# A four-layer graph network on one core: feature sums, weight sums and final additions given other places, some of them fixed, in the kernel's list of work

## The chip, the cores and the metric

The kernel runs on one core of one Trainium2 chip. The metric is the device time of one execution in microseconds (us). Before the change it is 2921.49 us, the median of four executions (2918.78 to 2921.88). The engines are PE (TensorE, matrix products), DVE (VectorE), ACT (ScalarE), POOL (GpSimd) and SP (SyncE, which here only issues DMAs); each works through a queue of its own in order.

## The reference, cut to what matters

There are N = 2708 nodes with 512 features in fp32 and one dense matrix `adj` of 2708 x 2708. Every layer multiplies a matrix made from `adj` with the features, and ends in a layernorm with a residual:

```python
x = _layernorm(x + _L0_gnn_ref(x, adj))        # (adj + row-normalised mask) @ x / degree
x = _layernorm(x + _L1_gnn_ref(x, adj, adj, ...))  # attention and GCN branch, gates
x = _layernorm(x + _L2_gnn_ref(x, adj, weight))
x = _layernorm(x + _L3_gnn_ref(x, adj, deg, W, b))

def _L2_gnn_ref(x, adj_norm, weight):
    out = x @ weight[0]
    p = x
    for idx in range(1, 4):
        p = adj_norm @ p
        out = out + p @ weight[idx]
    return out

def _L3_gnn_ref(x, adjacency, node_degree, W, b):
    dinv = jax.lax.rsqrt(node_degree)
    pooled = (dinv * (adjacency + eye) * dinv) @ x + x
    return jax.nn.relu(pooled @ W + b)
```

## The kernel before

**Tiling.** Each of the large products is cut into 2 x 2 blocks (two halves of 1354 nodes, two halves of 256 features) and done with seven block products in place of eight (Strassen's method in Winograd's form). That needs sums of blocks on both sides: for the features B11, B12, B21, B22 the sums T1 = B12 - B11, T2 = B22 - T1, T3 = B22 - B12 and T4 = B21 - T2, and for the matrix tiles the sums s1 to s4. All these sums are DVE instructions; the passes of the block products are PE's. In layers 0 and 1 the sums of the features are made once, whole, by `x_sums` (L220, L221, L223) and `x_last`, while the tiles of the layer before are still being normalised. The sums of the matrix tiles are made as the tiles arrive from memory (L396 there).

**Stages.** `S[0]` to `S[6]` are the starts of seven sweeps in a common list. Sweeps 0, 1 and 2 are done by `sweep` over ranges of 384, 384, 256 and 330 columns. Sweeps 3, 4 and 5 (the three hops of layer 2) and 6 (layer 3) are done by `sweep2`: it has two halves g of 676 and 678 columns, and in each of them seven products j = 0 to 6, each of 2 units of the list. A product is seven runs of passes (L1154), each run over 6 tiles of 128 rows in sweeps 3 to 5 and over 5 in sweep 6. Its runs use b11, t3, t1, t2, t4, b22 and b21 as the stationary side. The seven runs go into four PSUM banks: `accu`, `accc`, `accd`, `acca`. DVE needs, for one product: the sums s3, s1, s2 and the last one of the streamed tiles (`comb`, L1114); the sums t3, t1, t2, t4 of the stationary side (`tsum`, L1135, two instructions each); the additions that take the banks away (`leave`, L1178, with copies by ACT, L1172); additions among the products' results (`add`, L1190).

**The rest.** 1354 rows are 10 tiles of 128 and 74 more. The 74 last rows of both halves are multiplied on their own (`rest`, L1225 and L1229): eight passes into four banks `accr`, twice in the fourth product (j = 3) and twice in the sixth (j = 5) of half 0, and likewise in half 1. `rest_add` (L1236) adds the four banks to results on DVE, and that is what makes the banks free again. There are 8 PSUM banks in all.

**Other sums.** `ext_sums` makes the sums s1 to s4 of the transposed features that hop 2 and the others append to the matrix tiles (the sixth tile of a run): four loads from X2T by SP, four DVE sums (L1080), four stores by POOL's queue. It is called eight times, four in the sweep of S[2] and four in that of S[3].

**The end.** `done6` finishes layer 3. For the end group it takes the eight quarters (s, c) of the last product's result and does three DVE instructions on each (`pre`, L1334 to L1336: add the transposed features, multiply by the row factor, add again), then 6 tiles of dense products with the output weights (`ps_d`, L599), the bias and relu (L1359, L1360), and a layernorm (L548 to L558, with the power by POOL at L553).

**What sets the order.** Every piece of work is put into the list `events` by `at(pos, fn, hold)`. The list is sorted by `pos` and run, so that it gives the program's order. A scheduler then reorders the instructions of each engine by its own estimates, within the data dependences. Two things bind it: instructions before position START = 5.0 keep their order, and those of a `fn` recorded with `hold` are tied behind the instruction that stands before them in the list on their engine. The ties make no wait on another engine by themselves; they fix who stands behind whom in an engine's queue:

```python
p = last if n < 3 * strict else done if n in held else {}
if i.engine in p:
    tc.add_manual_dep(i, p[i.engine].name, ...)   # NoSync: "order of the list"
```

`x_sums`, `x_last` and `pre` are held before the change; `comb`, `tsum`, `leave`, `add`, `rest`, `rest_add` and `ext_sums` are not.

Of the kernel before, what the change touches and what calls it, by code (L numbers as in the profile page):

```python
# [24 lines left out]
ALU = mybir.AluOpType  # L25
P = 128
# [32 lines left out]
def wt(k):  # L59
    return min(P, NH - k * P) if k < KT else P  # L60
# [8 lines left out]
def gnn_kernel(ctx: ExitStack, tc: tile.TileContext, x, adjT, w_sa, a_sa, w_gcn, b_gcn, wab, bab, w_hop, w_out,  # L69
               b_out, out):  # L70
    nc = tc.nc
# [3 lines left out]
    HD = D // 2  # L75
# [41 lines left out]
    def feature(nm):  # L117
# [11 lines left out]
    X2T = {(g, h): dram.tile([D, 2 * n], F32, name=f"X2T{g}_{h}", tag=f"X2T{g}_{h}")  # L129
           for g, (_, n) in enumerate(RANGES2) for h in range(2)}  # L130
# [4 lines left out]
    SE = {(m, g, s): dram.tile([HD, n], F32, name=f"E{m}{g}{s}", tag=f"E{m}{g}{s}")  # L135
          for m in SUMS for g, (_, n) in enumerate(RANGES2) for s in range(2)}
# [4 lines left out]
    def move(queue, dst, src):  # L141

        m = dst.shape[0]
        c = m - m % 16 if m > 16 else m
        queue.dma_start(out=dst[:c], in_=src[:c])
        if c < m:
            queue.dma_start(out=dst[c:m], in_=src[c:m])

    def ring_tile(nm):
        return pool.tile([P, 384], F32, name=nm, tag="ring", bufs=RING)  # L150
# [21 lines left out]
    def at(pos, fn, hold=False):  # L172

        def go():
            n = len(nc.cur_bb.bb.instructions)
            fn()
            held.update(range(n, len(nc.cur_bb.bb.instructions)))

        events.append((pos, len(events), go if hold else fn))


    X = {}
# [8 lines left out]
    def new_x(s, k):  # L191
        X[s, k] = place(s, *HOME[k])
        return X[s, k]

    def place(s, g, i):
        if (s, g) not in groups or i in groups[s, g][1]:
            group(s, g)
        t, used = groups[s, g]
        used.add(i)
        return t if g == "R" else t[:, i, :]  # L200
# [12 lines left out]

    b12 = {}

    def x_sums(k):
        w = wt(k)
        b = b12.pop(k)
        b11, b22 = X["B11", k], X["B22", k]
        nc.vector.tensor_tensor(new_x("T1", k)[:w], b[:w], b11[:w], ALU.subtract)  # L220
        nc.vector.tensor_tensor(new_x("T2", k)[:w], b22[:w], X["T1", k][:w], ALU.subtract)  # L221
        X["T3", k] = b
        nc.vector.tensor_tensor(b[:w], b22[:w], b[:w], ALU.subtract)  # L223
        X.pop(("B12", k), None)
# [5 lines left out]
    def b12_tile(k):  # L230

        b12[k] = place("T3", *HOME[k])
        return b12[k]

    def x_source(src, k):

        lo, hi = src[k], src[KT + k]
        return lo[:, :HD], lo[:, HD:], hi[:, :HD], hi[:, HD:]

    def x_load(src, k, s, eng):  # L240
        w = wt(k)
        q = x_source(src, k)[("B11", "B12", "B21", "B22").index(s)]
        t = b12_tile(k) if s == "B12" else new_x(s, k)
        move(eng, t[:w], q)

    def next_x(base, src, sums=0.95, halves=-0.25):


        q = nc.gpsimd
        at(base + 1.3, lambda: rest_x(src, q))  # L250
        for k in range(KW):
            f = k / KT
            if (k * P) < RANGES[-1][0]:
                at(base - 5.8 + f, lambda k=k: x_load(src, k, "B11", q))
                at(base - 1.85 + f, lambda k=k: x_load(src, k, "B22", q))
                at(base - 1.84 + f, lambda k=k: x_load(src, k, "B12", q))
                at(base - 1.15 + f, lambda k=k: x_sums(k), True)
                at(base - 0.85 + f, lambda k=k: x_load(src, k, "B21", q))
                at(base + 1.5 + f, lambda k=k: x_last(k), True)
            else:  # L260
                at(base + halves + 0.05 * (k - 8), lambda k=k: x_load(src, k, "B22", q))
                at(base + max(halves, 0.1) + 0.05 * (k - 8), lambda k=k: x_load(src, k, "B21", q))
                at(base + sums + 0.03 * (k - 8), lambda k=k: x_sums(k), True)
                at(base + 2.6 + 0.03 * (k - 8), lambda k=k: x_last(k), True)
# [345 lines left out]
    S = [28.0 * s for s in range(8)]  # L610
# [172 lines left out]
    for k in range(KW):  # L783
        f = k / KT
# [80 lines left out]
    i = 0  # L865
# [200 lines left out]
            move(nc.gpsimd, o[b : b + m, :], src[t][a : a + m, :])  # L1066
        return o

    def ext_sums(g, s, q):

        n = RANGES2[g][1]
        E = {}
        for ij in ("11", "21", "22", "12"):
            E[ij] = ring_tile("a" + ij)
            e = (int(ij[1]) - 1) * HD + q * P
            nc.sync.dma_start(out=E[ij][:, :n], in_=X2T[g, int(ij[0]) - 1][e : e + P, s * n : (s + 1) * n])
        E["s3"] = ring_tile("s3")
        for m, o, a, b, op in (("s3", "s3", "11", "21", ALU.subtract), ("s1", "21", "21", "22", ALU.add),
                               ("s2", "11", "21", "11", ALU.subtract), ("s4", "12", "12", "11", ALU.subtract)):
            nc.vector.tensor_tensor(E[o][:, :n], E[a][:, :n], E[b][:, :n], op)  # L1080
            nc.gpsimd.dma_start(out=SE[m, g, s][q * P : (q + 1) * P, :], in_=E[o][:, :n])

    def sweep2(base, ext, done, extra=None):
        nk = K2 + ext
        u = 2 / 7
        for g, (i0, n) in enumerate(RANGES2):
            Q, C = {}, {}
            for j, m in enumerate(ORDER2[g]):
                b = base + 14 * g + 2 * j
                op, st = OPS2[m]  # L1090
# [46 lines left out]
                for nm, x, y, pos in (("t3", "b22", "b12", -0.9), ("t1", "b12", "b11", 0.1), ("t2", "b22", "t1", 0.9),  # L1137
                                      ("t4", "b21", "t2", 1.9)):
                    if g == j == 0:
                        pos = max(pos, 0.4)  # L1140
                    at(b + u * pos, lambda a=(nm, x, y), f=tsum: f(*a))

                def stat(v, k, T=T, st=st):
                    i, kk = k // 3, k % 3
# [12 lines left out]
                for i, (v, z, home, start) in enumerate((  # L1157
                        ("b11", (0, 0), "u", 1), ("t3", "s3", "c", 1), ("t1", (1, 0), "d", 1), ("t2", (0, 0), "u", 0),
                        ("t4", (1, 1), "c", 0), ("b22", (0, 0), "d", 0), ("b21", (0, 1), "a", 1))):
                    for k in range(nk):  # L1160
# [3 lines left out]
                src, dst = {(0, "Q6"): ("Q1", "Q1"), (0, "Q4"): ("Q1", "Q1"), (1, "Q6"): ("Q1", "U"), (1, "Q7"): ("U", "V"),  # L1164
                            (1, "Q4"): ("V", "V"), (1, "Q3"): ("U", "U"), (1, "Q2"): ("Q1", "Q1")}.get((g, m), (None, m))
# [72 lines left out]
            for j, pos, h, e, to in REST2[g]:  # L1238
                b = base + 14 * g + 2 * j
# [13 lines left out]


    for i in range(4):
        at(S[2] + 19.5 + 1.1 * i, lambda i=i: ext_sums(0, i // 2, i % 2))
        at(S[3] + 7.0 + 1.3 * i, lambda i=i: ext_sums(1, i // 2, i % 2))

    def hop_done(dst):

# [56 lines left out]
    def done6(p0, dp, g, i0, n, h, cc, tiles):  # L1317
        def rows(s):
            row[g, h, s] = ring_tile("row")
            nc.gpsimd.dma_start(out=row[g, h, s][:, :n], in_=bcast(DROW[h][0:1, i0 + s * n : i0 + (s + 1) * n], n))  # L1320

        x3T = {}

        end = (g, h) == (1, 0)

        def load_x3T(s, c):
            t = ring_tile("x3T")
            nc.gpsimd.dma_start(out=t[:, :n], in_=X3T[g, h, s][c * P : (c + 1) * P, :])
            x3T[s, c] = t

        def pre(s, c):
            t = x3T[s, c]
            y = cc(s, c)
            nc.vector.tensor_tensor(y[:, :n], y[:, :n], t[:, :n], ALU.add)  # L1334
            nc.vector.tensor_tensor(y[:, :n], y[:, :n], row[g, h, s][:, :n], ALU.mult)
            nc.vector.tensor_tensor(y[:, :n], y[:, :n], t[:, :n], ALU.add)  # L1336

        for s in range(2):
            at(p0 - (1.9 if end else 0.6), lambda s=s: rows(s))
            for c in range(DC):  # L1340
                if end:
                    a = p0 - 1.8 + 0.05 * c
                    b = p0 - 1.5 + 0.2 * (c - 2) + 0.4 * s if c >= 2 else p0 + {
                        (1, 1): -0.9, (1, 0): -0.6, (0, 1): -0.3, (0, 0): -0.07}[s, c]
                else:
                    a, b = p0 - 0.5 + 0.4 * s + 0.05 * c, p0 + 0.4 * s + 0.05 * c
                at(a, lambda s=s, c=c: load_x3T(s, c))
                at(b, lambda s=s, c=c: pre(s, c), True)
        for i, (s, lo, w) in enumerate(tiles[3:] + tiles[:3] if end else tiles):
            got = {}  # L1350
            r0 = i0 + s * n + lo

            def a(r0=r0, w=w, got=got):
                got["x"] = fetch2(X3, h, r0, w)

            def b(s=s, lo=lo, w=w, r0=r0, got=got):
                px = dense(lambda c: cc(s, c)[:, lo : lo + w], W[6], w)
                y = got["x"]
                nc.vector.tensor_tensor(px[:w], px[:w], vec[6][:w], ALU.add)  # L1359
                nc.vector.scalar_tensor_tensor(y[:w], px[:w], 0.0, y[:w], ALU.max, ALU.add)  # L1360
                layernorm([(y, 0, D)], y, w, True)
                move(nc.sync, out[h * NH + r0 : h * NH + r0 + w, :], y[:w])

            p = p0 - 0.095 + 0.14 * i if end else p0 + 0.4 + 0.25 * i
            at(p - 0.6, a)
            at(p, b)

    sweep2(S[6], 0, done6)

    strict = 0  # L1370
# [53 lines left out]
```

## Time and profile before

| | |
|---|---|
| median of four executions | 2921.49 us |
| the profiled execution's own time | 2921.88 us |
| its span, first to last instruction | 2919.8 us |
| PE busy | 2862.9 us, 98% of the span |
| DVE busy | 2236.2 us, 77% |
| POOL busy | 660.3 us, 23% |
| ACT busy | 579.5 us, 20% |
| mean granted TensorE clock | 0.995 |

The profile gives, for one execution, the busy time of each engine, groups of instructions by source line, the waits of each engine with what ended them, and a timeline of single instructions. Times inside the execution count from its first instruction. A line such as L1154 is a line of the kernel before; names such as `z` and `t` are the program's tiles with their numbers left out. A table of windows gives the busy time of each engine in a stretch, how many instructions it holds, and PEclk, the clock that TensorE was granted there (1.00 is full speed).

### The profile page before, as it was taken

The page shows a single profiled execution, that of the slowest core. Times are in us where ns is not written, and L with a number is a line of the kernel's source. Part 1 is how long each engine was busy: PE and PEld are TensorE (multiplying, and loading weights), DVE is VectorE, ACT ScalarE, POOL GpSimd, SP SyncE. Part 2 cuts the span into 40 slices and gives each one's busy share as a digit, 9 for nine tenths or more (in the row PEclk, how much of TensorE's full clock was granted, in tenths as well). Part 3 has the DMA queues.
Part 4 walks back from the last instruction along what each step waited for, and adds up shares of the span by engine and source line. Part 5 has one row for each costly group of instructions (what it writes and reads, how often), then busy time and mean ns, then how long its engine had stood idle before and what let it go on. Part 6 is the DMA issues. An engine that isn't in the chain of part 4 may idle for free. (4 is left out here: it accounts for less than half of the span.)

```text
span 2919.8 us, 37394 instructions
## 1 busy us (share of the span) xinstructions
PE 2862.9 (98%) x10846; PEld 1844.0 (63%) x10846; DVE 2236.2 (77%) x5676; ACT 579.5 (20%) x1133; POOL 660.3 (23%) x1178
## 2 busy tenths in 40 slices
PE   7999999999999999999999999999999999999998
PEld 5655665556665656866666666666666666655664
DVE  6898788566648675875789788887888878689887
ACT  4554200101137454651100000000000200100001
POOL 0133224113310101123113033030330413512202
PEclk9999999999999999999999999999999999999999
DMA  7665466444534333565677677576775776956652
GB/s 224 187 206 183 134 212 221 133 154 157 182 117 138 117 114 100 170 194 152 204 207 224 200 208 235 153 219 193 221 221 151 223 206 182 260 163 178 182 163 90
DMA packets 376248, 523.96 MB, mean 179 GB/s; under 512 B 64454, under 2 KB 326640, under 8 KB 376044
## 3 DMA queue, kind: packets, MB, share of 16 engines
q1 hardware_dynamic: 305688, 370.70, 43.6%
q0 software_dynamic: 53376, 139.76, 14.9%
q10 hardware_dynamic: 16980, 11.13, 1.4%
q8 instruction: 86, 1.41, 0.2%
q14 instruction: 118, 0.97, 0.1%
HBM read 432.14 MB, written 89.21 MB: 179 GB/s over the span
## 5 line engine op out<-in xcount | busy, mean ns | idle before, releaser
L1114 DVE TENSOR_TENSOR z<-z 128x339 f32<-128x339 f32 (+1 forms) x966 | 457.1, 504 | 15.0 <-PE accu L1154 3.8
L1172 ACT COPY q<-accu 128x338 f32<-128x338 f32 (+1 forms) x84 | 34.5, 443 | 986.5 <-PE accu L1154 986.5
L1154 PE MATMUL accu<-z,t 128*128 128x338 f32 (+1 forms) x644 | 195.8, 450 | 6.1 <-DVE q L1178 3.1
L1154 PE MATMUL accc<-s,t 128*128 128x338 f32 (+1 forms) x644 | 198.0, 450 | 0.0
L1154 PE MATMUL accc<-z,t 128*128 128x338 f32 (+1 forms) x644 | 196.1, 451 | 0.0
L1154 PE MATMUL accd<-z,t 128*128 128x338 f32 (+1 forms) x644 | 193.8, 448 | 1.4 <-DVE z L1114 1.4
L553 POOL TENSOR_TENSOR rstd<-rstd,neg_half 128x1 f32<-128x1 f32 (+3 forms) x92 | 62.2, 676 | 580.9 <-DVE rstd L552 578.2
L1275 POOL DMA_DIRECT2D Y<-y x192 | 105.2, 554 | 367.3 <-DVE y L1270 337.9
L396 DVE TENSOR_TENSOR a<-a,a 128x384 f32<-128x384 f32 (+2 forms) x330 | 161.6, 511 | 15.0 <-PE accu L451 14.4
L1154 PEld LDWEIGHTS accu<-z,t 128*128 128x128 f32 x644 | 122.1, 191 | 68.1 <-DVE z L1114 3.9
L1154 PEld LDWEIGHTS accc<-z,t 128*128 128x128 f32 x644 | 122.7, 192 | 62.3 <-issue 4.0
L1154 PEld LDWEIGHTS accd<-z,t 128*128 128x128 f32 x644 | 122.0, 190 | 62.8 <-DVE z L1114 1.9
L1154 PEld LDWEIGHTS accc<-s,t 128*128 128x128 f32 x644 | 120.3, 190 | 64.1 <-issue 8.3
L1114 DVE TENSOR_TENSOR s<-z 128x338 f32<-128x338 f32 (+1 forms) x322 | 150.3, 504 | 12.3 <-PE accc L1154 8.4
L1178 DVE TENSOR_TENSOR q<-q,accd 128x338 f32<-128x338 f32 (+1 forms) x112 | 56.3, 503 | 128.2 <-PE accd L1154 128.2
L972 ACT ACTIVATE e<-row,neg_s 128x384 f32<-128x384 f32 (+5 forms) x176 | 100.4, 571 | 80.1 <-DVE e L974 25.4
L974 DVE TENSOR_TENSOR e<-e,f 128x384 f32<-128x384 f32 (+5 forms) x176 | 87.5, 506 | 28.5 <-ACT f L973 27.8
L973 ACT ACTIVATE f<-row,neg_s 128x384 f32<-128x384 f32 (+5 forms) x176 | 100.0, 568 | 24.4 <-PE accc L451 5.1
L599 PE MATMUL ps_d<-w,q 128*128 128x512 f32 (+2 forms) x192 | 86.2, 595 | 1.8 <-DVE ld L1360 1.3
L399 POOL DMA_DIRECT2D As<-a x120 | 64.9, 544 | 93.1 <-DVE a L396 78.1
L890 DVE SCALAR_TENSOR_TENSOR deg<-a,deg 128x384 f32<-128x384 f32 (+2 forms) x152 | 75.4, 504 | 13.3 <-DMA a<-in_adjT 12.1
L975 DVE SCALAR_TENSOR_TENSOR a<-a,e 128x384 f32<-128x384 f32 (+2 forms) x160 | 80.2, 507 | 4.1 <-DMA a<-in_adjT 1.9
(609 smaller groups left out, 5933.6 us busy)
## 6 DMA issues: line engine op xcount, KB each, us to landing
z<-As SPq DMA_DIRECT2D x320, 169.5 KB
z<-As SPq DMA_DIRECT2D x320, 169.0 KB
a<-in_adjT SPq DMA_DIRECT2D x240, 192.0 KB
z<-in_adjT SPq DMA_DIRECT2D x240, 169.5 KB
z<-in_adjT SPq DMA_DIRECT2D x240, 169.0 KB
a<-in_adjT SPq DMA_DIRECT2D x120, 165.0 KB
a<-in_adjT SPq DMA_DIRECT2D x112, 128.0 KB
As<-a POOLq DMA_DIRECT2D x60, 192.0 KB, 3.5
```

The costliest lines, as they stand in the source:

```text
L396: nc.vector.tensor_tensor(A[r, dst, k][:, :n], A[r, a, k][:, :n], A[r, b, k][:, :n], op)
L399: nc.gpsimd.dma_start(out=SD[m][k * P : (k + 1) * P, R0 : R0 + n], in_=A[r, dst, k][:, :n])
L553: nc.gpsimd.tensor_tensor(rstd[:w, 1:2], rstd[:w, 0:1], neg_half[:w], ALU.pow)
L599: nc.tensor.matmul(o, lhs(c), r, start=c == 0 and n == 0, stop=c == DC - 1, skip_group_check=True)
L890: nc.vector.scalar_tensor_tensor(d[:w, :n], a[:w, :n], 0.0, d[:w, :n], ALU.not_equal, ALU.add)
L972: nc.scalar.activation(e[:w, :n], row[R0, h][0][:w, :n], AF.Exp, bias=neg_s[:w, t : t + 1])
L973: nc.scalar.activation(f[:w, :n], row[R0, h][1][:w, :n], AF.Exp, bias=neg_s01[:w, t : t + 1])
L974: nc.vector.tensor_tensor(e[:w, :n], e[:w, :n], f[:w, :n], ALU.min)
L975: nc.vector.scalar_tensor_tensor(a[:w, :n], a[:w, :n], 0.0, e[:w, :n], ALU.not_equal, ALU.mult)
L1114: nc.vector.tensor_tensor(d[:, :n], Z[x + (k,)][:, :n], Z[y + (k,)][:, :n], op)
L1154: nc.tensor.matmul(B[home][:, :n], stat(v, k), a[:, :n], start=bool(start and k == 0), stop=k == nk - 1, skip_group_check=True)
L1275: nc.gpsimd.dma_start(out=rows[:, :, f * P : (f + 1) * P], in_=o[32 * f : 32 * (f + 1), : m * P].rearrange("p (b d) -> p b d", d=P))
```

## The change

It has four parts, and no instruction is added or removed: the number of instructions of every engine is the same.

1. **Feature sums of a layer** (`next_x`): `x_sums` is cut in two. The first of the three sums, T1 (L220), becomes `x_first` and is put, for the eight tiles of the ranges before the last, at `base - 2.3` in place of `base - 1.15`; it stays held. The loads of B12 go from `base - 1.84` to `base - 3.2`.
2. **Extension sums** (`ext_sums`): the four loads stay at their place; the four sums come 0.9 units later and are held; the four stores come 0.9 units later.
3. **Sums of the dense side** (`tsum`): held in half 0 for the products j = 0 to 3, in sweeps 3 to 6. Their positions don't change.
4. **The final additions** (`pre` of `done6`, for the end group): (0, 2), (1, 2), (0, 3), (1, 3) go from `p0 - 1.5`, `-1.1`, `-1.3`, `-0.9` to `p0 - 0.5`, `-0.7`, `-0.4`, `-0.65`, and (1, 1) from `p0 - 0.9` to `p0 - 0.75`. The three others stay.

```diff
+    def x_first(k):
+        w = wt(k)
+        nc.vector.tensor_tensor(new_x("T1", k)[:w], b12[k][:w], X["B11", k][:w], ALU.subtract)
+
+    def x_sums(k, first=True):
         w = wt(k)
+        if first:
+            x_first(k)
         b = b12.pop(k)
...
-                at(base - 1.84 + f, lambda k=k: x_load(src, k, "B12", q))
-                at(base - 1.15 + f, lambda k=k: x_sums(k), True)
+                at(base - 3.2 + f, lambda k=k: x_load(src, k, "B12", q))
+                at(base - 2.3 + f, lambda k=k: x_first(k), True)
+                at(base - 1.15 + f, lambda k=k: x_sums(k, False), True)
...
+        at(pos, loads)
+        at(pos + 0.9, sums, True)
+        at(pos + 0.9, stores)
...
-                    at(b + u * pos, lambda a=(nm, x, y), f=tsum: f(*a))
+                    at(b + u * pos, lambda a=(nm, x, y), f=tsum: f(*a), g == 0 and j < 4)
...
-        at(S[2] + 19.5 + 1.1 * i, lambda i=i: ext_sums(0, i // 2, i % 2))
-        at(S[3] + 7.0 + 1.3 * i, lambda i=i: ext_sums(1, i // 2, i % 2))
+        ext_sums(S[2] + 19.5 + 1.1 * i, 0, i // 2, i % 2)
+        ext_sums(S[3] + 7.0 + 1.3 * i, 1, i // 2, i % 2)
...
-                    b = p0 - 1.5 + 0.2 * (c - 2) + 0.4 * s if c >= 2 else p0 + {
-                        (1, 1): -0.9, (1, 0): -0.6, (0, 1): -0.3, (0, 0): -0.07}[s, c]
+                    b = p0 + {(1, 1): -0.75, (1, 2): -0.7, (1, 3): -0.65, (1, 0): -0.6, (0, 2): -0.5, (0, 3): -0.4,
+                              (0, 1): -0.3, (0, 0): -0.07}[s, c]
```

## The prediction

> **What bounds the kernel now.** I read the page's first part, then PE's waits, then the windows around each wait, and last the timeline of DVE there. PE is busy 98% of the span, so time can be won only where PE stands still or runs at half clock, and be lost wherever a sum now comes too late for it. The waits of PE (engine, line, what it waited for, us in total, times, longest):
>
> ```profile
> PE accr L1225 <- DVE q L1236: 4.7, 2, 4.4
> PE ps_n L582 <- DVE P1c L512: 3.9, 1, 3.9
> PE accu L1154 <- DVE q L1178: 3.1, 1, 3.1
> PE accd L1154 <- DVE z L1114: 3.0, 5, 1.4
> PE accu L1154 <- DVE z L1114: 3.0, 1, 3.0
> ```
>
> Each of them is a wait for DVE, which is busy 77% on the whole: DVE does the right work in the wrong order. The reader is to see single long waits, not many short ones. What a long wait costs besides is in the windows (PE's busy time, then PEclk, the granted clock):
>
> ```profile
> 439.10:442.51 3.41, 1.11 (x4) 0.36 (x2) 3.41 (x11) 0.00 (x0) 1.50 (x4) 1.00 0.98 358
> 442.51:445.92 3.41, 1.80 (x6) 1.27 (x7) 3.41 (x10) 0.00 (x0) 3.41 (x7) 0.50 0.44 126
> 445.92:449.34 3.42, 3.42 (x10) 2.10 (x9) 3.09 (x6) 0.00 (x0) 3.42 (x7) 0.50 0.79 266
> ```
>
> After a stretch of 3.41 us in which PE was busy 1.11 us, two stretches run at half clock. The same follows at 374.25 (busy 1.49), 1534.78 and 2558.78 (busy 1.50), but not at 2872.80 (busy 1.66, idle 1.75). So I price a half-clock stretch at half of what PE was busy in it, and say that it comes from about 1.9 us of idle in a stretch.
>
> The Trainium skill, "TensorE: Matmul & The Clock Gate", Part 1, says that the clock falls after at least one idle window of about 3.4 us. By that rule none of the stretches above (idle at most 3.27 us, at 1534.78) would halve the clock, my three terms for it (0.9, 1.7 and 1.7 us) would be nothing, and the sum below would be 4.3 us less. The rows speak against it, and they decide.
>
> **Part 1, feature sums, 440 us.** PE waits 3.91 us (440.21 to 444.12) for P1c (L512), which DVE reaches at 443.58. Between 428.8 and 441.7 DVE does seven of the T1 sums (L220) at a pitch of 0.335 us, 2.35 us in all. They move to 404 to 416, where DVE is busy 9.48 of 12 us and waits 2.42 us at 410.24; their inputs are there by then, because the loads' queue (POOL) keeps its order. Then P1c comes about 2.0 us sooner and the wait is 1.9 us. Loss at half clock now: (1.80 + 3.42)/2 = 2.6 us; 1.9 us of idle is on the edge, so one such stretch may stay, and I count 0.9 (bounds 0 and 2.6). Together 2.9 us.
>
> **Part 2, extension sums, 1533 us.**
>
> ```profile
> 1520.09 0.51 DVE L1178 TENSOR_TENSOR q<-q,accd 128x338 f32<-128x338 f32 x1 [1.11 <-PE accd L1154]
> 1525.91 0.51 DVE L1080 TENSOR_TENSOR s<-a,a 128x339 f32<-128x339 f32 x1 [5.31 <-DMA a<-X2T]
> ...
> 1537.49 1.75 DVE L1236 TENSOR_TENSOR q<-q,accr 128x338 f32<-128x338 f32 x4
> ```
>
> DVE stands 5.31 us behind a sum whose loads have not landed, with everything else queued behind it, and so frees the bank of the rest 4.43 us too late. With the sums 0.9 units (about 11 us) later and tied there, DVE is 3 to 5 us earlier at L1236 (1532.6 to 1534.3) and the wait goes. With it goes a half-clock stretch in which PE was busy 3.50 us: 4.43 + 1.7 = 6.1 us. The four stores also come later on POOL's queue; POOL is busy 4.18 of 4.50 us at 1533.6 and 2.42 of 3.50 after, and their reader, the next half of the hop, is far. In layer 2's last range (1280 to 1330) the same tie, and the order that the scheduler builds around it, makes DVE wait some 8 us for `accd` (L512); counting 45 sums at 0.43 us after that, the sum C21 reaches PE 0.3 us late. I count -0.3.
>
> **Part 3, stationary sums held.** This cuts both ways.
>
> Gain, sweep 6. At 2535 to 2565 DVE is late for two PE waits, 1.39 us at 2555.08 and 3.00 at 2560.28:
>
> ```profile
> 2540.45 0.43 DVE L1135 TENSOR_TENSOR t<-B11D,B11B 128x256 f32<-128x256 f32 x1 [4.90 <-DMA B11D<-X]
> ...
> 2547.47 0.51 DVE L1178 TENSOR_TENSOR q<-q,accu 128x338 f32<-128x338 f32 x1 [2.81 <-ACT q L1172]
> ```
>
> The t3 sum, unheld, stands ahead of the leaves and waits 4.90 us for its load; then ACT's copy, behind a slow store, costs 2.81. Held, t3 goes behind the leave of `accd` (PE done at 2545.3), and the layernorm chain ahead of it no longer waits for t sums. Laid end to end from 2545.3 at the pitches of the timeline (0.42 for a 338-column sum, 0.87 for 768 columns, 0.47 and 0.34 for t), the z sums are ready 0.65 us late for the first wait and, with PE taking seven passes of the next banks ahead, 0.9 us late for the second. The 0.59 us at 2504.68 goes too. Gaps: 0.6 + 0.7 + 2.1 = 3.4. Half clock now: (2.33 + 3.41)/2 = 2.9; 0.65 + 0.9 = 1.55 us of idle is below the 1.75 that kept full clock, but not by much, so I count only the longer stretch, 1.7 (bounds 0 and 2.9). Together 5.1 us. If ACT's copy stays late, the second wait stays 3.0 and 3.8 of this is gone.
>
> Loss, the start of the fourth product in sweeps 3 to 6, where the rest runs. Now, in sweep 3:
>
> ```profile
> 1467.55 0.51 DVE L1178 TENSOR_TENSOR q<-q,accd 128x338 f32<-128x338 f32 x1 [0.85 <-PE accd L1154]
> 1467.97 0.55 DVE L1135 TENSOR_TENSOR t<-T2C,T2A 128x384 f32<-128x384 f32 x1
> ...
> 1470.30 2.19 DVE L1114 TENSOR_TENSOR s<-z 128x338 f32<-128x338 f32 x5
> ...
> 1476.38 1.75 DVE L1236 TENSOR_TENSOR q<-q,accr 128x338 f32<-128x338 f32 x4
> ```
>
> In the new order the leaves and even the first L1236, which must wait for PE's eighth rest pass (1474.7), stand ahead of s3. DVE stands still for some 3 us before it. s3 comes at 1475.7, PE wants it at 1475.3: 0.5 us. Then the second L1236, which frees the bank of the last rest pass, stands behind ten s and z sums (0.42 us each) and four t sums (0.47): 14 instructions after the first, done at 1481.75, where PE arrives at 1480.35: 1.4 us. The 0.26 us wait at 1463.00 goes. Net 1.65 us, and the same rows stand in sweeps 4 and 5 (waits of 0.26 at 1830.68 and 2191.94); in sweep 6, by the same count, 1.55. Sum 6.5 us. The two idle times lie 4.8 us apart, so I expect no half clock. Bounds: 0, if PE's passes are enough ahead, and 2 x 1.7 us more per boundary if the clock falls.
>
> At the other product starts (j = 1, 2) the first s3 is ready 4.8 us before PE wants it (in sweep 4: 1787.1 against 1791.9). Held sums cost nothing there; that cover is what the second rival takes away.
>
> **Part 4, the end.** PE waits 0.84 us at 2886.00 for a z sum (L1114), and the six passes before it take 2.34 us where six later ones take 1.87, since DVE deals z sums and final additions in turn. With nine of these additions behind the z sums, PE reaches the 48 output passes (0.43 us each, 20.9 us, no waits) 0.8 + 0.6 = 1.4 us sooner, and DVE's last needed addition is done by 2890.0 instead of 2891.3. After them all is a chain, so 1.4 us is won (bounds 0 and 1.5). The 3.09 us wait at 2874.46 is behind POOL's power (L553); nothing moves there.
>
> **Sum.** 2.9 + 6.1 - 0.3 + 5.1 - 6.5 + 1.4 = 8.7 us. From the profiled execution's own 2921.88 us (span 2919.8) that gives 2913.2; its own time lies 0.4 above the median of the runs, which I leave out.
>
> **Rivals.**
> 1. **No difference that can be measured: 2918.** The clock stays low behind the shorter waits (0.9 and 1.7 us less) and in sweep 6 ACT's copy is still late (2.1 less): 8.7 - 4.7 = 4.0. For it: 1.9 us of idle stands at the edge, and POOL's stores set that copy. Against it: DVE's waits for t go in any case. Chance 0.25.
> 2. **Slower: 2930.** The held t sums make DVE wait for `accd` at each of the other held product starts as well, and s3 comes late. It decides from 4.8 us of delay; then the second stall of 1.4 us comes at some 12 more starts, 17 us: 2913.2 + 17 = 2930. For it: a tied instruction holds up all that stands behind it, as L1080 does above for 5.31 us. Against it: those starts have no rest, so no L1236 stands in the queue. Chance 0.10.
> 3. **The boundaries cost nothing: 2906.7.** DVE and PE make up the 1.65 us by waits that go elsewhere. Chance 0.15; the forecast has 0.50.
>
> **How the numbers follow.** About 0.2%, 5.8 us, is what a measurement of this kernel can tell from no change, so "faster" means below 2916.1 (from the profiled time). The forecast's own spread reaches over that bound with about 0.05 of the chance: faster 0.45 + 0.15 = 0.60, same 0.05 + 0.25 = 0.30, slower 0.10. The range, 2906 to 2920, holds the forecast and rivals 1 and 3 and leaves out the slower one.
>
> **What will show it.** Right: PE's wait for L1236 at about 1533 gone; the wait for P1c about 2 us; no half clock at 1538; first output pass 1.4 us sooner relative to the last products; new PE waits of 0.5 and 1.4 us at `accc` L1174 and `accr` L1245 (the new numbers of L1154 and L1225) once in each of sweeps 3 to 6. Wrong: new waits at j = 1 and 2, half clock in sweeps 3 to 6, or DVE waiting for DMA at the moved extension sums.

## The result, and the profile after

The changed kernel takes 2924.76 us (median of 34 executions, 2920.77 to 2929.67), the kernel before 2920.65 us (55 executions); the ratio is 1.0017, 95% interval 1.0012 to 1.0022. That is 3.5 to 6.4 us slower, where 8.7 us faster was forecast, and above the range of 2906 to 2920. It is just inside the 0.2% that I had named as what a measurement of this kernel can tell from no change. The profiled execution took 2925.11 us with a span of 2923.2.

PE's waits in the changed kernel, in the columns of the waits shown before (the page's own line of busy times first):

```profile
PE 2861.9 (98%) x10846; PEld 1841.4 (63%) x10846; DVE 2235.9 (76%) x5676; ACT 579.8 (20%) x1133; POOL 659.6 (23%) x1178
```
```profile
...
PE accu L1174 <- DVE q L1198: 3.6, 1, 3.6
PE accr L1245 <- DVE q L1256: 3.5, 4, 1.1
PE accc L1174 <- DVE s L1134: 3.0, 3, 1.0
PE rs L711 <- DVE run L698: 2.3, 1, 2.3
...
PE ps_n L588 <- DVE P1c L518: 1.5, 1, 1.5
PE accc L1174 <- ACT q L1192: 1.4, 1, 1.4
```

The waits that the change aims at are gone or short: 4.4 us for L1236 (now L1256) at 1533, 3.9 us for P1c, now 1.5. In their place stand new ones: 1.0 us for a streamed sum and 1.1 us for the bank of the rest, three times each (sweeps 3, 4 and 5), 2.3 us for the row sums of layer 2 (`rs`), 1.4 us for a copy by ACT in sweep 6. These are lines of PE in the changed kernel at 440 us, behind it, and at 1533 us (no wait):

```profile
439.32 0.73 PE L588 MATMUL ps_n<-ident,P1c 128*128 128x128 f32 x2 [1.55 <-DVE P1c L518]
...
452.61 1.56 PE L457 MATMUL accu<-a,B11D 128*128 128x384 f32 x4 [0.67 <-DVE B11D L566]
...
485.22 0.27 PE L854 MATMUL ps_r<-ident,rdeg 128*3 128x128 f32 x1 [0.72 <-DVE s L846]
...
1535.30 2.44 PE L1245 MATMUL accr<-r,B11R 116*128 116x338 f32 x8
```

To see what each place costs, I matched every PE pass of one trace with the pass of the same tiles in the other and read how far it is shifted. The shift is flat between the places that matter, so its steps are a ledger in us (minus is earlier), the forecast beside it:

| place | forecast | measured |
|---|---|---|
| up to 400 us, nothing changed there | 0 | -2.4 |
| layer 0 to 1 (440) | -2.9 | -2.9 |
| layer 2's last range (1260 to 1340) | +0.3 | +4.9 |
| fourth product of sweeps 3, 4, 5 | +1.65 each | +3.7 each |
| rest of sweep 3 (1533) | -6.1 | -6.4 |
| sweep 6 (2500 to 2610) | -5.1 + 1.55 | -2.5 |
| the end (2870 on) | -1.4 | +1.6 |
| sum | -8.7 | +3.4 |

The last pass of PE is 3.3 us later; the other -0.1 is in steps below 0.4. The difference of the spans is 3.4. The first row is how two executions differ where their work and order are the same: one and then no half-clock stretch near 100 and 378 us where the profile before has two and one.

### The profile page after: what moved, and what is told of

It is laid out like the page before. It is cut to its first block, busy times and chain, and to the rows that moved or that the text cites. A ratio compares the mean times of both kernels' runs of the same rounds, so it can differ in the third digit from the quotient of the medians.

```text
span 2923.2 us, 37397 instructions
## 1 busy us (share of the span) xinstructions
PE 2861.9 (98%) x10846; PEld 1841.4 (63%) x10846; DVE 2235.9 (76%) x5676; ACT 579.8 (20%) x1133; POOL 659.6 (23%) x1178
## 4 chain that ended last, share of the span: by engine, by line
PE 84%; DVE 6%; issue 4%; DMA 3%; POOL 1%; ACT 1%; SPq 0%; POOLq 0%; DVEq 0%; ACTq 0%
PE accu L1174 11%; PE accd L1174 11%; PE accc L1174 11%; PE ps_d L605 9%; PE accc L457 8%; PE accd L457 8%; PE accu L457 7%; PE acca L1174 5%; PE acca L457 4%; PE accr L1245 2%; DVE z L1134 1%; PE accr L1249 1%; PE acca L466 1%; PE accd L466 1%; PE ps_t L594 1%
## 5 line engine op out<-in xcount | busy, mean ns | idle before, releaser
L1192 ACT COPY q<-accu 128x338 f32<-128x338 f32 (+1 forms) x84 | 34.5, 443 | 994.7 <-PE accu L1174 897.0
```

## The experiments

In these kernels one part is undone or done alone. Where a time is given as a ratio, it is to the kernel before, run on the same chip in the same session, with its 95% interval. The changed kernel (1.0017, 1.0012 to 1.0022) did not run again beside them, so it is compared by way of these ratios; and the traces are of several chips, on which the kernel before took 2920.65 to 2924.89 us.

**Each part undone.** Four kernels, the changed one with one part put back: `x_sums` whole at `base - 1.15` and the B12 loads at -1.84; `ext_sums` in one piece at `pos`; `tsum` without hold (its edit is shown); `pre` at the old positions.

```diff
-                    at(b + u * pos, lambda a=(nm, x, y), f=tsum: f(*a), g == 0 and j < 4)
+                    at(b + u * pos, lambda a=(nm, x, y), f=tsum: f(*a))
```

> The changed kernel with part 1 undone (the T1 sums of the features back at their old place). Theory A (every part has its own place, and what the two traces show there adds up): the wait for P1c at 440 us is back at about 3.9 us with its half-clock stretches, and the time is 2.9 us above that of the changed kernel. Theory B (what follows in a sweep moves with the feature sums, so that the gain is given back later): within 1 us of the changed kernel.

Measured: 1.0030 (1.0018 to 1.0041), 0.13% (3.8 us) above the changed kernel, the intervals overlapping. The wait for P1c is back at 4.2 us. The shift against the changed kernel's trace is +4.3 us at that place, of which 1.8 go again by 490, where two waits of 0.7 us that part 1 had brought (lines at 452 and 485 above) are absent. That leaves +2.5. Theory A.

> The changed kernel with part 2 undone (extension loads, sums and stores together again, not held). Theory A: the 4.9 us lost between 1260 and 1340 go (DVE no longer waits 7.7 us for ACT there, and the 2.3 us wait of PE for the row sums is gone), and the 6.4 us won at 1533 go as well, so the time is about 1.5 us above the changed kernel. Theory B (the loss at 1260 to 1340 comes of part 1, whose order puts PE 5 us ahead of DVE): the loss stays, and the time is 6 us above the changed kernel.

Measured: 1.0033 (1.0020 to 1.0045). The row sums' wait falls from 2.3 to 0.4 us and the wait for L1256 at 1535 is 3.2 us again, with half clock behind it: the shift goes by -4.2 us at 1250 to 1330 and by +6.4 from 1330 to 1545. So both the loss in layer 2 and the gain at 1533 are part 2's, as theory A says. The time alone doesn't decide: it is 0.16% or 4.7 us above the changed kernel, A said 1.5 and B 6, and the intervals overlap. In the trace 1.7 us more come in sweep 4 and 3.5 in sweep 6, where part 2 moves nothing.

> The changed kernel with part 3 undone (the t sums free for the scheduler in all sweeps). Theory A (the tie is the cause of the new waits at the fourth product): the new waits of 0.6, 1.0 and 1.1 us in sweeps 3, 4 and 5 go, 3 times 3.7 us; the gain of sweep 6 (2.5 us) goes too: 8 to 9 us below the changed kernel. Theory B (those waits come of DVE being late from part 2's tie, not from part 3): they stay in sweep 3 and the time is 2 us or less below the changed kernel.

Measured: 0.9975 (0.9965 to 0.9986), 0.42% or about 12 us below the changed kernel. The new waits in sweeps 3 to 5 are gone, and the shift falls by 3.6 us at each. Theory A, but it is more than A's 8 to 9 us, and the trace doesn't show where the rest is: three times 3.6 us are 10.8, and sweep 6 gives back 2.5 of them, as A said.

> The changed kernel with part 4 undone (the final additions at their old places). Theory A (part 4 wins 1.4 us at the end, and the loss there in the profiled execution, 1.4 us of half clock after a wait of 3.6 us, belongs to POOL's order and to where the clock's stretches fall): the time is 1 to 1.5 us above the changed kernel, and PE waits 0.8 us for a z sum near the end again. Theory B (part 4 makes the 3.1 us wait longer): the time is 1 to 2 us below the changed kernel.

Measured: 1.0025 (1.0016 to 1.0034), 0.08% above the changed kernel, intervals overlapping. PE's wait for POOL's chain ahead of the end is 3.8 us, no shorter than with part 4 (3.6), so theory B is out; but no wait of 0.8 us for a z sum came back either, so theory A isn't shown.

**Which ties cost the fourth product its waits.** `j < 4` becomes `j == 3` in one kernel and `j < 3` in the other.

> The changed kernel with the t sums held in half 0 for the fourth product only (j = 3). Theory A (DVE comes late to the fourth product because the ties at j = 1 and 2 made it wait for PE, about 5 us, while it still had 30 us of feature sums ahead; the tie at j = 3 alone costs little more than the order forecast): the waits at the start of the fourth product in sweeps 3 to 5 fall from 3.7 to 2 us or less per sweep, the 0.6 us wait ahead of them goes, and with the free sums of j = 1 and 2 sweep 6 is as in the kernel with all t sums free; ratio to the kernel before about 0.999. Theory B (the tie at j = 3 itself is the whole cause): 3.7 us per sweep as in the changed kernel, ratio about 1.001.

> The changed kernel with the t sums held in half 0 for j = 0 to 2 and free at j = 3. Theory A: DVE is still about 5 us late when the fourth product starts, PE still waits there, 1.5 to 3 us per sweep in sweeps 3 to 5, and sweep 6 still waits for ACT's copies; ratio about 1.000. Theory B: no new wait in sweeps 3 to 5; ratio about 0.998.

Measured: 0.9974 (0.9965 to 0.9983) with the tie at j = 3 alone, just as with no tie, and 1.0006 (0.9997 to 1.0015) with the ties at j = 0 to 2. With j = 3 alone none of the new waits stands in sweeps 3 to 5, and DVE's order there is that of the kernel before, but for one addition that changes places with a t sum; with j = 0 to 2 waits of 0.6 and 0.8 us stand in each. So my term's cause was wrong, and theory B too: by itself the tie where the waits are costs nothing.

What the ties at j = 2 do is in DVE's timeline of the changed kernel at the start of the third product:

```profile
1434.78 0.51 DVE L1198 TENSOR_TENSOR q<-q,accu 128x338 f32<-128x338 f32 x1 [0.31 <-ACT q L1192]
1437.37 0.51 DVE L1198 TENSOR_TENSOR q<-q,accc 128x338 f32<-128x338 f32 x1 [2.08 <-PE accc L1174]
1440.79 0.51 DVE L1198 TENSOR_TENSOR q<-q,accd 128x338 f32<-128x338 f32 x1 [2.90 <-PE accd L1174]
1441.21 0.55 DVE L1155 TENSOR_TENSOR t<-B11C,B11A 128x384 f32<-128x384 f32 x1
```

In the kernel before, the same t sum starts at 1432.21, and the s sums at 1436.33:

```profile
1432.21 0.55 DVE L1135 TENSOR_TENSOR t<-B11C,B11A 128x384 f32<-128x384 f32 x1
...
1436.33 1.77 DVE L1114 TENSOR_TENSOR s<-z 128x338 f32<-128x338 f32 x4 [0.38 <-PE accc L1154]
```

Tied, DVE waits 5 us for PE with nothing to do, since the sums that it could do stand behind the leaves. That is not yet a loss for PE, as forecast. At the second product DVE is as late (its s sums start 5.8 us later), but there it is level again at 1431, since in the kernel before it waits 6.4 us for PE at that place. Behind the third product come the sums of the next layer's features (L351 to L354, 0.95 us each), and from 1441 to 1474 DVE has one gap, of 0.28 us, in which to make up for it: T4D ends at 1468.1 instead of 1462.8. No run ties j = 2 alone in these sweeps; that it is this tie and not j = 1 is read from the two timelines. At the fourth product it is still late, and there PE waits. PE's timeline of the changed kernel there (start, duration, in brackets the wait before):

```profile
1474.74 0.85 PE L1249 MATMUL accr<-r,B22R 32*128 32x338 f32 x8
1476.60 2.54 PE L1174 MATMUL accc<-s,t 128*128 128x338 f32 x8 [1.00 <-DVE s L1134]
1478.97 1.87 PE L1245 MATMUL accr<-r,B21R 116*128 116x338 f32 x6
1480.77 0.84 PE L1249 MATMUL accr<-r,T1R 32*128 32x338 f32 x6
1482.68 0.84 PE L1245 MATMUL accr<-r,B21R 116*128 116x338 f32 x2 [1.06 <-DVE q L1256]
1483.44 0.83 PE L1249 MATMUL accr<-r,T1R 32*128 32x338 f32 x2
```

The two waits have the places and about the sizes that I forecast (0.5 and 1.4), but with 0.6 us ahead of them at 1458, and with the eight passes of the rest torn apart: the last two passes and the last two 32-row passes go alone. That makes 3.7 us of the 1.65.

**Layer 2's last range, and a better kernel.** The first kernel keeps parts 1 and 4, leaves the t sums free, and does part 2 for the four sums in the sweep of S[3] only. In the second the loads of the S[2] group come later too; in the third that group is later but not held; in the fourth held but not later.

In the edit of the first kernel `both` does the loads, sums and stores of a group in one piece, as before the change, and g == 0 is the group of S[2]:

```diff
+        if g == 0:
+            at(pos, both)
+            return
         at(pos, loads)
         at(pos + 0.9, sums, True)
         at(pos + 0.9, stores)
```

> Parts 1 and 4, part 2 for the four extension sums of the sweep of S[3] only (the four of S[2] as before), t sums free. Theory A: the 4.9 us that the changed kernel lost between 1260 and 1340 do not arise (no wait of 2 us for the row sums, no half clock behind it), all else as in the kernel with the t sums free (ratio 0.9975): ratio 0.9958. Theory C (that loss comes of part 1): ratio 0.9975 again, and the wait for the row sums is still there.

> As the kernel with the t sums free, but in the sweep of S[2] the loads of the extension sums come 0.6 units later as well, so that their five ring tiles are held for 0.3 units in place of 0.9 before the sums; the sums stay 0.9 later and held. Theory A (the tiles that wait for their sums take places of the ring, and ACT and DVE wait for places): the DVE wait of 7.7 us behind ACT's exponentials near 1275 goes and the time is that of the kernel with those sums as before, ratio 0.9958. Theory D (the place of the held sums in DVE's queue is the cause): the loss stays, ratio 0.9975.

> As the kernel with the t sums free (part 3 undone), but the four extension sums of the sweep of S[2] stand 0.9 units later without being held. Theory D1 (the tie is what changes the order around 1260 to 1340): the wait of about 2 us for the row sums and the half-clock stretch behind it go, ratio 0.996. Theory D2 (the later place alone makes the scheduler deal the work of ACT and DVE in the other order): the wait stays, ratio 0.9975.

> As the kernel with the t sums free, but the extension sums of the sweep of S[2] keep their old place (no 0.9 units) and are held there. Theory D1 (the tie): the wait of about 2 us for the row sums stays, ratio 0.9975. Theory D2 (the place): it goes, but DVE may wait for the loads as a tied sum does, some 3 us at a time; ratio 0.996 if nothing is late by that.

Measured:

| kernel | ratio | longest DVE wait for ACT's f | PE's wait for the row sums |
|---|---|---|---|
| t sums free (later, held) | 0.9975 (0.9965 to 0.9986) | 7.7 us | 2.1 us |
| w1, S[2] group as before | 0.9960 (0.9947 to 0.9972) | 2.7 | 0.8 |
| w2, loads later too | 0.9979 (0.9970 to 0.9988) | 7.7 | 2.3 |
| x1, later, not held | 0.9966 (0.9953 to 0.9978) | 7.7 | 0.7 |
| x2, held, not later | 0.9960 (0.9948 to 0.9973) | 3.9 | 0.8 |

w1 is about 12 us below the kernel before, and nothing that I ran is clearly better; x1, x2 and two kernels below can't be told from it by their times. The time that tiles wait in the ring is not the cause (w2 shortens it and keeps the wait). The later place brings the 7.7 us wait with it, with or without the tie (x1); the place and the tie together bring the 2.1 to 2.3 us wait of PE. That is read from the traces; the intervals of the times overlap. That wait ends a stretch in which PE is busy 1.16 of 3.42 us, and half clock follows (windows of the changed kernel, columns as before):

```profile
1319.30:1322.72 3.42, 1.16 (x9) 0.98 (x9) 3.42 (x10) 0.61 (x1) 0.00 (x0) 0.99 0.93 288
1322.72:1326.14 3.42, 3.42 (x14) 1.68 (x12) 3.42 (x17) 0.00 (x0) 0.00 (x0) 0.51 0.77 254
```

And the 7.7 us are these two lines of the changed kernel's timeline: ACT's copy of a dense product, which waits for PE, stands ahead of the exponentials that DVE waits for.

```profile
1272.12 0.59 ACT L1037 COPY y<-ps_d 128x512 f32<-128x512 f32 x1 [3.96 <-PE ps_d L605]
...
1275.38 0.50 DVE L980 TENSOR_TENSOR e<-e,f 128x330 f32<-128x330 f32 x1 [7.74 <-ACT f L979]
```

**Part 4, and the tie in sweep 6**, each against w1: part 4 undone; the t sums held for sweep 6, half 0, j = 2 only.

> The best kernel so far (parts 1 and 4, part 2 for S[3] only, t sums free) with part 4 undone. If part 4 wins its 1.4 us at the end, the time is 1.4 us above that kernel, ratio 0.9965, with a wait of 0.8 us for a z sum near the end. If it wins nothing, ratio 0.996.

> The best kernel so far with the t sums of the third product of sweep 6 held, and no others. As I forecast part 3's gain: the waits of 0.8 and 3.0 us near 2550 shrink to 0.65 and 0.9, with less half clock, ratio 0.9945. Theory ACT (in the held order the next thing in DVE's queue is an addition that waits for ACT's copy, which stands behind ACT's copy for the transposed features, which waits for a store that POOL issues late): a new wait of 1.4 to 4 us ahead of the old place, ratio 0.996 or above.

Measured: 0.9964 (0.9951 to 0.9976) without part 4, and 0.9954 (0.9940 to 0.9967) with the tie. Neither can be told from w1's 0.9960. In the traces the shift between w1 and x4 is 2.1 us at 2565 and 1.9 at the last pass: part 4 wins nothing there. In w1 PE even waits 0.7 us for one of the moved additions ahead of the output passes; in x4 it doesn't. With the tie the 0.8 us wait falls to 0.3 but the wait of 3.0 us stays.

In the changed kernel DVE's tied order waits for ACT:

```profile
2543.24 0.59 ACT L596 COPY xT<-ps_t 128x512 f32<-128x512 f32 x1 [6.35 <-DMA X3T<-xT]
2543.73 0.45 ACT L1192 COPY q<-accc 128x338 f32<-128x338 f32 x1
2549.60 0.44 ACT L596 COPY xT<-ps_t 128x332 f32<-128x332 f32 x1 [5.42 <-DMA X3T<-xT]
2549.93 0.79 ACT L1192 COPY q<-accu 128x338 f32<-128x338 f32 x2
```

The copies that DVE's additions need (L1192) stand behind copies of transposed features (L596), which wait until a store has landed and freed their tile. POOL issues that store late, behind loads that wait in turn for other stores to land (3.7 us ahead of 2536.70). To see whether this sets PE's 3.0 us, two kernels let ACT's own queue issue the store, with the tie and without it:

```diff
-                store_T(X3T[g, h, s][:, lo : lo + w], transposed(...)[:, :, :w])
+                store_T(X3T[g, h, s][:, lo : lo + w], transposed(...)[:, :, :w], nc.scalar)
```

> The kernel with the tie at the third product of sweep 6, and the transposed features stored by ACT's own queue right after its copy, in place of POOL's. Theory ACT (my forecast gain in sweep 6 failed because DVE's tied order stands behind ACT's copies, which stand behind a store that POOL issues late): DVE's wait of about 6 us for ACT's copy at the third product goes, the 3.0 us wait of PE near 2550 falls to about 1 us and the half-clock stretches behind it go; ratio 0.993 to 0.994. Rival (DVE is simply full there): the 3.0 us wait stays, ratio 0.9955.

> The same change of the store on the kernel without any tie of t sums. Theory ACT: the order without the tie still waits for the load of the third product's features, so the 3.0 us wait stays or falls little; ratio 0.995 to 0.996. Rival: the store alone wins what there is to win, ratio 0.994 as with the tie.

Measured: 0.9981 (0.9972 to 0.9990) and 0.9980 (0.9971 to 0.9989), slower than without it. The 3.0 us wait near 2550 is gone in both, with and without the tie. But a wait of 2.1 and 2.6 us for the same copy of ACT now stands at 2531, with half clock behind it: there are two tiles for the transposed features, and the copy waits 3.9 us until a store has freed one (x7):

```profile
2532.75 0.44 ACT L596 COPY xT<-ps_t 128x332 f32<-128x332 f32 x1 [3.90 <-DMA X3T<-xT]
2533.21 0.37 ACTq L614 DMA_DIRECT2D X3T<-xT  x1
2533.62 0.44 ACT L1201 COPY q<-accc 128x338 f32<-128x338 f32 x1 [0.44 <-ACT xT L596]
```

This wait spoils the test. PE comes to the place near 2550 5.3 us later in x7 than in w1, more than its two waits there in w1 (0.8 and 3.0 us), and from 2538 on DVE does the same work in the two kernels within 0.02 us. So PE's own lateness is enough to take the waits away. What the store did remove is DVE's wait of 2.2 us for ACT's copy at 2538 in w1. With the tie DVE waits longer for ACT, 8.0 us in x6 where x5 has 4.6 and 6.1, so that part of the expectation failed, and so did mine for x7 that the wait stays. Whether ACT's and POOL's lateness or DVE's full queue sets the 3.0 us stays open.

At the last pass of PE x7 stands 0.1 us behind w1, and x6 0.3 ahead of x5. What the two kernels lose they lose behind the issue of the last store of the output: the span ends 6.7 us after it, and 2.2 us in w1 and x5.

## Why the prediction was wrong

**Part 1** held in its mechanism; that its number did, -2.9 us forecast and -2.9 in the ledger, is luck. The wait for P1c was 1.5 us, not 1.9, and both half-clock stretches behind it went, where I had counted one in part. That moved PE 4.6 us, and 1.8 came back at 452 and 485, where PE, being earlier, now waits 0.7 us twice.

**Part 2 at 1533** held: -6.1 forecast, -6.4 measured, and +6.4 when undone. DVE no longer waits for X2T there; relative to PE it comes to L1256 4.9 us earlier.

**Part 2 in layer 2** failed: "the sum C21 reaches PE 0.3 us late" was +4.9. I started DVE's count at a wait of 8 us for `accd` and took every instruction from there at its pitch. That wait isn't in the run. There DVE had lost 3.2 and 7.7 us at 1267 and 1275, some 50 us before PE's wait, waiting for PE and ACT, because the scheduler had put ACT's dense copies ahead of its exponentials. I had compared DVE's order with PE's, and looked neither at ACT's nor at what stood before the stretch. I had also left PE at its old times, though part 1 let it come earlier; but that is not the cause, since the wait is 2.5 us with part 1 undone. What was late was the row sums, not C21. Of the 4.9 us the wait is 2.3; most of the rest is the half-clock stretch behind it.

**Part 3 at the fourth product** failed in its cause, and with it in its size: +1.65 per sweep was +3.7. The step that failed is "Held sums cost nothing there; that cover ...": I had set 4.8 us of cover against the first s sum and stopped counting. The 5 us that DVE lost at j = 2 did not reach PE there; they were carried through 33 us in which DVE is full, to the fourth product. The tie that I priced, at j = 3, costs nothing by itself (0.9974 against 0.9975). My second rival named the right ties, and was wrong in where they would tell.

**Part 3 in sweep 6** failed: -5.1 was forecast for the two waits at 2555 and 2560. The waits of DVE for loads went, as forecast, but DVE then waited for ACT's copies, 4.9 and 3.9 us in the changed kernel's trace; "if ACT's copy stays late" was the condition that I named and left out of the sum. PE's waits are no shorter for it: 1.4 and 3.0 us before, 1.4, 2.0 and 1.3 after, the last with no cause in the profile. The 2.5 us of the ledger are the two half-clock stretches that did not come, and that was luck: one stretch, at 2558.31, has PE busy 1.53 us. In four other kernels with these ties (u1, u2, u4, and h012 without that at j = 3) PE waits 3.5 to 3.9 us for ACT there, with half clock behind it.

**Part 4** failed in size: -1.4 forecast; +0.08% and +0.04% when undone, either way within the intervals, and 0 in the traces of w1 and x4. In the changed kernel the 0.84 us wait is gone and the passes behind it come 1.5 us sooner, but the wait of 3.1 us ahead of them became 3.6, and half clock behind it cost 2.6 us; that is the +1.6 of the ledger. The 1.5 us can't be called part 4's either: in u4 and x4, where the wait ahead is 3.8 and 4.0 us, the wait for the z sum isn't there with the old order. What sets the length of the wait ahead (2.4 to 4.5 us in these traces) between the kernels was not found: POOL's power stands behind loads there in all of them.

**Half clock.** I took it to follow from about 1.9 us of idle in a stretch. In every trace the half-clock stretches start on one grid of 3.413 us (in the kernel before 377.66, 442.51, 1538.19 and 2562.19). Counted on these grids over all sixteen traces, my rule is nearly right: a stretch at full clock with PE busy 1.50 us or less was followed by half clock in 70 of 70 cases, one with 1.87 or more in 3 of some 13,300, and the 26 between went both ways. By my rule the new waits at the fourth product should not have brought half clock, and the three exceptions are there: with PE busy 2.36 us in the stretch at 1479.70 the changed kernel kept full clock; with the same busy time u1, u2 and u4 lost it behind these waits. What decides between them stays open. This is u1:

```profile
1483.14:1486.55 3.41, 2.35 (x11) 0.90 (x10) 3.41 (x9) 0.00 (x0) 0.00 (x0) 1.00 0.47 141
1486.55:1489.97 3.42, 3.42 (x7) 1.95 (x7) 3.33 (x8) 0.00 (x0) 0.00 (x0) 0.50 0.59 132
```

The Trainium skill, "TensorE: Matmul & The Clock Gate", Part 1, describes a window that runs freely and doesn't start with the kernel; that agrees with the grids. Its measure of a whole idle window doesn't agree with these rows.

The sum: the three places where I followed one engine only (layer 2, the fourth products, sweep 6) miss by 4.6, 6.2 and 1.1 us and the end by 3.0; together 14.9 us, against which stand the 2.4 us at the start that no change made and 0.3 at 1533.

## What to carry to other kernels

An instruction tied to its place in an in-order queue holds up all that could have filled the wait: ask of each tie what DVE would otherwise have done in that time, and follow the lateness on to the next place where the engine is not full, rather than to the first reader. When a scheduler builds the order, compare the order of every engine (here ACT's) over the whole stretch, not only that of the two engines in the wait. A change of several parts is worth taking apart: here part 1 and part 2 in one of its two sweeps (part 4 adds nothing that can be told) win 12 us together, and the rest of the change gave all of it back.

## What the runs showed of the hardware

The eight passes of 32 rows at the end of a rest overlap: all eight take 0.85 us; six take 0.84. Two that are left alone take 0.83 us, so splitting such a group costs about the time of the whole group.

Issuing some of the late stores from ACT's queue made the execution end 6.7 us after the issue of its last output store instead of 2.2 us, though these stores had landed long before. No run shows why.
